# Layer 0 of a four-layer graph network in source order, with other numbers of buffers

## The chip, the cores and the metric

The kernel runs on one core of one Trainium2 chip. The metric is the device time of one execution in microseconds. TensorE (PE) multiplies matrices into PSUM, VectorE (DVE) does elementwise work and reductions, ScalarE (ACT) does activations and copies, GpSimd (POOL) issues the indirect gathers, and SyncE (SP) issues most of the other loads. Each engine works through its own queue in order. ACT issues stores as well.

## The reference, cut to what matters

A graph of 12,500 nodes with 64 features and 212,500 edges passes through four layers: a graph attention layer (layer 0), three graph convolutions (layer 1), five rounds of an edge network (layer 2) and a mean aggregation (layer 3). A residual sum and a normalization follow each. Layer 0 is this:

```python
h = (x @ W).reshape(n, HEADS, CH)                      # 4 heads of 16
e = leaky_relu(a_src[src] + a_dst[dst], 0.2)           # one value per edge and head
m = segment_max(e, dst); e = exp(e - m[dst])
s = segment_sum(e, dst)
out = segment_sum(h[src] * (e / s[dst])[:, :, None], dst)
y = layernorm(x + out + bias) * gamma + beta           # then layernorm(x + y)
```

Each self loop is added as an edge of its own.

## The kernel before

The nodes are cut into 128 windows of 98 (`NQ`, `QB`). The edges that end in a window lie in 128 x 16 slots: 14 columns hold rows gathered by matmuls with one-hot matrices and stored to DRAM beforehand, two hold overflow rows that POOL gathers. Windows go in groups of four (`G`). First the edges are sorted into slots and the rows for layer 0 are gathered; then the layers follow, each in a phase with its own pools of buffers.

For each window d, layer 0 does the following.

- `fetch` loads the gathered rows `hg` (one SP load and two POOL gathers). The features and the source's attention terms of every edge are in it.
- `place` builds the one-hot matrix of slots against nodes in two halves (`h32` on VectorE, a copy `hot` in FP8 on ScalarE, stored to `hot_d`), multiplies the attention terms by the edge's rank among those of its node (`rh`, `rv`) and adds them up per node and rank in PSUM (`prank`, 8 matmuls per half). TensorE runs a float32 matmul as two instructions, so the trace has 16 per half.
- `largest`, once per group, takes the largest attention value of each node from `prank`, the number of edges, and the term of the self loop (`pself`).
- `attend` builds the other one-hot matrix (`ot`), spreads the largest value back over the edges (`pd`, 16 matmuls), forms the exponent in a chain of small VectorE instructions (`ad`, then four on `z`), takes Exp on ScalarE, and multiplies the rows: `msg`.
- `add_up_whole` turns `hot` to float32 (`o32`, ScalarE) and adds up the messages per node in PSUM (`pacc`, 16 matmuls).
- `node0`, once per group, divides, adds the residuals, normalizes twice, and makes the table of layer 1: transposes and a dense matmul on TensorE (`pnode`), `tnew` on VectorE, then for each of the four windows a gather block (42 matmuls into `pgat`, two copies to `hb` on ScalarE, stores to `g_d`).
- `pump(6)` has POOL gather six columns of edge attributes for layer 2, which TensorE transposes (`pattr`) and ScalarE copies and stores.

POOL and SP follow the order of the source everywhere in the network. In layer 0 and layer 2, PE, ACT and DVE follow an order that a planner sets when the program is built, from a cost model of its own; in layers 1 and 3 they follow the source order (`tc.manual_schedule`). The source of layer 0 has `place` for window d, then `attend` and `add_up_whole` for window d-4, and at the end of a group the whole of `node0` and of `largest`. A layer 1 pass (`run_pass`) works in steps: each step does its window and then one piece of each node generator that is going.

Buffer numbers are given with the tiles: `hg` 9 in layer 0 (`hgbufs`), 7 in layers 1 and 2, 6 in layer 3; `hb` 2 in layer 0 (`hbbufs`), 4 later; the table `tnew` 2; `pacc`, `pd` and `prank` one each.

Of the kernel before, what the change touches and what calls it, by code (L numbers as in the profile page):

```python
# [865 lines left out]
def tile_gnn_resnorm_d4(ctx: ExitStack, tc: tile.TileContext, a: dict, out: bass.AP):  # L866
# [455 lines left out]
    def network():  # L1322
        with ExitStack() as s0:
# [77 lines left out]
            def inv_sqrt(val, shape, name):  # L1401
                sd = nw.tile(shape, F32, name=name + "_s")
                r = nw.tile(shape, F32, name=name + "_r")
                sca.activation(sd, val, AF.Sqrt)
                v.reciprocal(r, sd)
                v.tensor_mul(sd, r, r)
                v.tensor_mul(sd, sd, val)
                v.tensor_scalar(sd, sd, -0.5, 1.5, op0=OP.mult, op1=OP.add)
                v.tensor_mul(r, r, sd)
                return r  # L1410

            def layernorm(y, dst, gamma=None, beta=None):
                s = nw.tile([QB, G], F32, name="ln_sum")
                v.tensor_reduce(out=s, in_=y, axis=AX.X, op=OP.add)
                v.tensor_scalar(s, s, -1.0 / D, None, op0=OP.mult)
                v.tensor_tensor(y, y, s[:, :, None].to_broadcast([QB, G, D]), op=OP.add)
                sq = nt("ln_sq", bufs=1)
                v.tensor_mul(sq, y, y)
                va = nw.tile([QB, G], F32, name="ln_var")
                v.tensor_reduce(out=va, in_=sq, axis=AX.X, op=OP.add)  # L1420
                v.tensor_scalar(va, va, 1.0 / D, LN_EPS, op0=OP.mult, op1=OP.add)
                r = inv_sqrt(va, [QB, G], "ln")
                rb = r[:, :, None].to_broadcast([QB, G, D])
                if gamma is None:
                    v.tensor_tensor(dst, y, rb, op=OP.mult)
                else:
                    v.tensor_tensor(y, y, rb, op=OP.mult)
                    v.tensor_tensor(y, y, wide(gamma), op=OP.mult)
                    v.tensor_tensor(dst, y, wide(beta), op=OP.add)
# [103 lines left out]
            def add_up_whole(hot, x, ps):  # L1533

                nj = NJ // 2
                for hf in range(2):
                    o32 = wk.tile([P, nj, P], F32, name="o32", bufs=o32bufs)
                    sca.copy(o32, hot[:, hf * nj:hf * nj + nj, :])
                    for j in range(nj):
                        pe.matmul(ps, lhsT=o32[:, j, :], rhs=x[:, hf * nj + j, :], start=(hf + j == 0),  # L1540
                                  stop=(hf == 1 and j == nj - 1))
# [68 lines left out]
            def table():  # L1610
                return nw.tile([QB, 3, G, D], F32, name="tnew")
# [14 lines left out]
            hgbufs, ohbufs, hbbufs, o32bufs = 2 * G + 1, G + 2, 2, 2  # L1626
# [6 lines left out]
            def place(d, i, pk, hg, hot):  # L1633


                rh = wk.tile([P, RANKS, NJ], BF16, name="rh", bufs=1)
                v.tensor_tensor(rh, rk[:, d, None, :].to_broadcast([P, RANKS, NJ]), iotr, op=OP.is_equal)
                nj = NJ // 2
                for hf in range(2):
                    js = slice(hf * nj, hf * nj + nj)  # L1640
                    h32 = wk.tile([P, nj, P], F32, name="h32", bufs=3)
                    v.tensor_tensor(h32, dl[:, d, js][:, :, None].to_broadcast([P, nj, P]),
                                    iotb[:, None, :].to_broadcast([P, nj, P]), op=OP.is_equal)
                    sca.copy(hot[:, js, :], h32, saturate=False)
                    rv = wk.tile([P, nj, RANKS * H + 1], F32, name="rv")
                    v.tensor_tensor(rv[:, :, :RANKS * H].rearrange("p j (r h) -> p j r h", h=H),
                                    rh[:, :, js].rearrange("p r j -> p j r")[:, :, :, None].to_broadcast([P, nj, RANKS, H]),
                                    hg[:, js, D:][:, :, None, :].to_broadcast([P, nj, RANKS, H]), op=OP.mult)
                    v.memset(rv[:, :, RANKS * H:], 1.0)  # L1649
                    for j in range(nj):  # L1650
                        pe.matmul(pk[:, i // 2, i % 2, :RANKS * H + 1], lhsT=h32[:, j, :], rhs=rv[:, j, :],  # L1651
                                  start=(hf + j == 0), stop=(hf == 1 and j == nj - 1))
                sca.dma_start(hot_d[d], hot.rearrange("p j e -> p (j e)").bitcast(F32))
# [29 lines left out]
            def attend(hg, db, a3):  # L1683
                ot = wk.tile([QB, NJ, P], BF16, name="ot", bufs=1)
                v.tensor_scalar(ot, db, pcol[:QB], None, op0=OP.is_equal)
                pd = ps_tile([P, NJ, 3, 2 * H], "pd")
                for j in range(NJ):
                    pe.matmul(pd[:, j, :, :], lhsT=ot[:, j, :], rhs=a3, start=True, stop=True)
                ad = wk.tile([P, NJ, 2 * H], F32, name="ad")
# [8 lines left out]
                sca.activation(msg[:, :, D:], z, AF.Exp)  # L1698
                v.tensor_tensor(heads(msg[:, :, :D]), heads(hg[:, :, :D]),  # L1699
                                msg[:, :, D:][:, :, :, None].to_broadcast([P, NJ, H, C]), op=OP.mult)  # L1700
                return msg

            def node0(g, xsum, acc, ps, t0, x0):
# [13 lines left out]
                layernorm(y, y2, gamma0, beta0)  # L1717
                v.tensor_add(y2, y2, x0)
                x1 = nt("x1")
                layernorm(y2, x1)  # L1720
                deg = nw.tile([QB, G], F32, name="deg4")
                v.tensor_scalar(deg, cnt[:, sl], 1.0, None, op0=OP.add)
                v.tensor_copy(dinv[:, sl], inv_sqrt(deg, [QB, G], "dg"))
                for _ in conv(g, x1, ws1[0], 0, (x_d, x1)):
                    pass
# [33 lines left out]
            def load_db(d):  # L1759
                db = wk.tile([QB, NJ, P], BF16, name="db", bufs=3)  # L1760
# [3 lines left out]
            held = []  # L1764
# [3 lines left out]
            for d in range(NQ + G):  # L1768

                g, i = divmod(d, G)  # L1770
                if d + G - 1 < NQ:
                    held.append([fetch(d + G - 1, DH, g0_d, t0_d)])
                if d < NQ:
                    if i == 0:
                        pk = ps_tile([P, G // 2, 2, 256], "prank")
                    hot = wk.tile([P, NJ, P], F8, name="hot", bufs=G + 2)
                    held[d].append(hot)
                    place(d, i, pk, held[d][0], hot)
                    pump(6)
                if G - 2 <= d < NQ + G - 2:  # L1780
                    held[d - G + 2].append(load_db(d - G + 2))
                if d >= G:
                    if i == 0:
                        t0 = state(t0_d, g - 1, "t0", DH)
                        x0 = nt("x0")
                        load_x(x0, G * (g - 1))
                        xsum = nt("xsum", DH)
                    if i == 0:
                        ps = ps_tile([P, G, DH], "pacc")
                    hg, hot, db = held[d - G]  # L1790
                    add_up_whole(hot, attend(hg, db, a3[:, :, i]), ps[:, i, :])
                    if i == G - 1:
                        node0(g - 1, xsum, ps, pself, t0, x0)
                if d < NQ and i == G - 1:
                    a3, pself = largest(g, pk)
# [3 lines left out]
            hgbufs, ohbufs, hbbufs = AHEAD + 3, 2 * G, 4  # L1799
# [206 lines left out]
```

## Time and profile before

| | |
|---|---|
| Time, median of 11 runs | 11348.07 us (11321.43 to 11371.93) |
| The profiled execution: its time, its span | 11338.61 us, 11336.7 us |
| Busy: PE, DVE, ACT, POOL | 77%, 77%, 32%, 55% |
| Mean granted TensorE clock | 0.866 |
| Layer 0, about 1650 to 3510 us | PE 85% busy, DVE 79%, ACT 49%, POOL 73%, DMA share 0.51 |
| Layer 1, about 3510 to 5640 us | PE 71%, DVE 65%, POOL 71%, DMA share 0.89 |
| Layer 2, about 5640 to 10660 us | PE 94%, DVE 82%, POOL 44%, DMA share 0.72 |

How to read it: a group of instructions is named by its line in the kernel, its engine, its operation and output<-input; a line can be that of a helper that several callers share. A row of stretches gives, for each engine, the busy time and the number of instructions, then the clock that TensorE was granted (1.00 is full speed), the mean busy share of the 16 DMA engines, and GB/s. A wait names the instruction that waited, the one that released it, the total in us, how often, and the longest. A timeline row gives start, duration, engine, line and operation. Releasers are inferred, so a wait for several things is put down to the last.

### The profile page before, as it was taken

Reading aid. Unit: us, or ns where it says so; the run is one execution under the profiler, and the core shown is the slowest. Engines: PE = TensorE matmul, PEld = TensorE weight load, DVE = VectorE, ACT = ScalarE, POOL = GpSimd, SP = SyncE. Lnnn points to the kernel's source line nnn. Section 1 sums busy time; section 2 is a strip of 40 time slices with the busy share of each in tenths; the row PEclk is TensorE's granted clock in tenths of the full one; section 3 lists DMA queues with packets and bytes.
Section 4 is the critical chain, followed back from the end, with each engine's and each line's share of the span. In section 5 each row is a group of like instructions: output and inputs, shape, how many; then the busy total and the mean of one; then the engine's idle time right before and its main releaser. Section 6 shows DMA issues by size and latency. Waiting matters only on the chain.

```text
span 11336.7 us, 260322 instructions
## 1 busy us (share of the span) xinstructions
PE 8707.2 (77%) x101921; PEld 7312.9 (65%) x102115; DVE 8752.0 (77%) x16365; ACT 3652.6 (32%) x6423; POOL 6246.8 (55%) x4616
## 2 busy tenths in 40 slices
PE   2332468888886766677799999999998999898761
PEld 2110468888886666666677777777776777777551
DVE  6889447887775656667678878887887887888898
ACT  2341234544442222222233333333333333233200
POOL 0667578877765777776344434434443443444460
PEclk9855668988887888878799999999999999999885
DMA  2663684555456999988777767767776776767671
GB/s 79 223 225 105 190 255 136 171 149 154 146 154 192 291 283 294 294 266 276 233 246 233 238 211 239 237 203 248 236 237 212 238 238 197 244 226 236 202 231 51
DMA packets 1377992, 2414.81 MB, mean 213 GB/s; under 512 B 421097, under 2 KB 732537, under 8 KB 1376625
## 3 DMA queue, kind: packets, MB, share of 16 engines
q1 hardware_dynamic: 734770, 1565.65, 43.4%
q10 hardware_dynamic: 494495, 714.10, 17.5%
q0 software_dynamic: 147488, 118.29, 6.8%
q8 instruction: 808, 13.24, 0.5%
q14 instruction: 431, 3.53, 0.1%
HBM read 1655.94 MB, written 741.25 MB: 211 GB/s over the span
## 4 chain that ended last, share of the span: by engine, by line
PE 26%; DVE 14%; DMA 10%; issue 4%; ACT 2%; ACTq 1%; SPq 1%; POOL 0%; DVEq 0%; POOLq 0%
PE pacc L1530 7%; PE pe L1859 6%; PE p L1840 6%; PE pgat L931 4%; DVE msg L1524 3%; DMA hot<-hot_d 2%; DMA g_d<-hb 2%; DVE msg L1864 2%; DMA et<-at_d 1%; DVE hg L1524 1%; DVE eh L1439 1%; DMA oh<-oh_d 1%; DMA hg<-g_d 1%; ACT hb L932 1%; PE pe L1854 1%
## 5 line engine op out<-in xcount | busy, mean ns | idle before, releaser
L1496 POOL DMA_INDIRECT hg<-tq_d,q_ovr x2304 | 3378.1, 1466 | 3480.0 <-DVE msg L1864 1422.3
L959 POOL DMA_INDIRECT ag<-in_edge_attr_dram,q_eid x2048 | 2532.7, 1237 | 992.7 <-issue 573.6
L1530 PEld LDWEIGHTS <-hot 128*128 128x128 fp8e4 x18432 | 1715.0, 103 | 693.9 <-issue 538.3
L932 ACT COPY hb<-pgat 128x448 f32<-128x448 f32 (+1 forms) x2560 | 1301.2, 535 | 2172.7 <-PE pgat L931 1222.4
L931 PEld LDWEIGHTS <-oh 98*128 98x128 fp8e4 x48384 | 1751.4, 101 | 281.0 <-issue 255.9
L931 PE MATMUL pgat<-tnew,oh 98*128 98x64 bf16 x48384 | 1811.9, 198 | 151.7 <-ACT hb L932 104.0
L1524 DVE TENSOR_TENSOR msg<-msg 128x1024 f32<-128x1024 f32 x1280 | 1561.7, 1220 | 7.7
L1859 PEld LDWEIGHTS pe<-we,eh 128*128 128x128 f32 x10240 | 1364.2, 193 | 249.8 <-issue 116.1
L1859 PE MATMUL pe<-we,eh 128*128 128x128 f32 x10240 | 1478.9, 281 | 21.1 <-DVE eh L1439 8.6
L1438 ACT ACTIVATE eh<-p,be 128x512 f32<-128x512 f32 x1280 | 869.3, 687 | 1902.5 <-PE p L1840 1335.2
L1840 PE MATMUL p<-et,we 128*128 128x512 f32 x2560 | 1298.2, 609 | 123.0 <-DMA et<-at_d 67.6
L1524 DVE TENSOR_TENSOR hg<-hg 128x1024 f32<-128x1024 f32 x1024 | 1249.7, 1226 | 120.5 <-DMA hg<-tq_d,q_ovr 46.4
L1530 PE MATMUL pacc<-hg,hot 128*128 128x192 bf16 x8192 | 970.2, 282 | 360.8 <-DVE hg L1524 185.3
L1530 PE MATMUL pacc<-msg,hot 128*128 128x192 bf16 x10240 | 1042.6, 248 | 36.9 <-DVE msg L1524 26.6
L1864 DVE TENSOR_TENSOR msg<-pe,hg 128x512 f32<-128x512 f32 x1280 | 868.1, 686 | 243.0 <-PE pe L1859 233.4
L1439 DVE SCALAR_TENSOR_TENSOR eh<-eh 128x512 f32<-128x512 f32 x1280 | 862.5, 685 | 201.2 <-ACT eh L1438 200.9
L1651 PE MATMUL prank<-rv,h 128*128 128x161 f32 x4096 | 732.4, 336 | 128.9 <-DVE rv L1649 74.8
L1651 PEld LDWEIGHTS prank<-rv,h 128*128 128x128 f32 x4096 | 664.4, 216 | 143.6 <-DVE rv L1649 100.8
L1178 PE MATMUL taken<-sg,hotc 128*128 128x456 bf16 x512 | 245.3, 556 | 551.4 <-ACT sg L1175 447.1
L1840 PEld LDWEIGHTS p<-et,we 128*128 128x128 f32 x2560 | 427.9, 194 | 340.9 <-issue 139.1
L1540 PE MATMUL pacc<-msg,o 128*128 128x68 f32 x4096 | 580.3, 309 | 76.0 <-DVE msg L1699 74.9
L1540 PEld LDWEIGHTS pacc<-msg,o 128*128 128x128 f32 x4096 | 564.5, 224 | 88.8 <-DVE msg L1699 65.4
(321 smaller groups left out, 9724.8 us busy)
## 6 DMA issues: line engine op xcount, KB each, us to landing
hg<-g_d SPq DMA_DIRECT2D x1152, 448.0 KB
g_d<-hb ACTq DMA_DIRECT2D x1152, 416.0 KB
hot<-hot_d SPq DMA_DIRECT2D x1152, 256.0 KB
oh<-oh_d SPq DMA_DIRECT2D x1152, 171.5 KB
et<-at_d SPq DMA_DIRECT2D x640, 256.0 KB
vb<-vw_d SPq DMA_DIRECT2D x128, 912.0 KB
hg<-g_d SPq DMA_DIRECT2D x128, 476.0 KB
g_d<-hb ACTq DMA_DIRECT2D x128, 442.0 KB
```

The lines of the kernel that those rows point to most:

```text
L931: pe.matmul(ps[:, j, :], lhsT=oh[:, 7 * hf + j, :], rhs=t3(k), start=(k == 0), stop=(k == 2))
L932: sca.copy(hb[:, 7 * hf:7 * hf + 7, :], ps)
L959: pool.indirect_dma_start(out=ag[:, j, :], out_offset=None, in_=a["edge_attr_32"], in_offset=bass.IndirectOffsetOnAxis(ap=eid[:, d, lo + j ...
L1439: v.scalar_tensor_tensor(dst, dst, 0.1, dst, op0=OP.mult, op1=OP.max)
L1496: pool.indirect_dma_start(out=hg[:, NG + i, :], out_offset=None, in_=tab, in_offset=bass.IndirectOffsetOnAxis(ap=ovr[:, d, i:i + 1], axis= ...
L1524: v.tensor_tensor(x[:, k + 1], x[:, k], top[:, k], op=OP.subtract)
L1530: pe.matmul(ps.rearrange("p (k f) -> p k f", k=3), lhsT=hot[:, j, :], rhs=top[:, :, j, :], start=(j == 0), stop=(j == NJ - 1))
L1540: pe.matmul(ps, lhsT=o32[:, j, :], rhs=x[:, hf * nj + j, :], start=(hf + j == 0), stop=(hf == 1 and j == nj - 1))
L1651: pe.matmul(pk[:, i // 2, i % 2, :RANKS * H + 1], lhsT=h32[:, j, :], rhs=rv[:, j, :], start=(hf + j == 0), stop=(hf == 1 and j == nj - 1))
L1840: pe.matmul(p1.rearrange("p q e -> p (q e)"), lhsT=w["we1"][:, j].rearrange("p t d -> p (t d)"), rhs=et, start=True, stop=True)
L1859: pe.matmul(ps[:, u:u + 2, :].rearrange("p t d -> p (t d)"), lhsT=h1[j][:, (2 * hf + q) * P:(2 * hf + q + 1) * P], rhs=w["we2"].rearrange( ...
L1864: v.tensor_tensor(msg[:, half, :], ps, hg[:, half, :], op=OP.mult)
```

## The change

Layer 0's phase runs PE, ACT and DVE in source order, and its source becomes a loop of steps. Step d fetches for window d+3, places window d, makes the messages of window d-5 and the sums of window d-6, and runs one piece of every node generator that is going. `place`, `attend`, `node0` and the normalization become generators with yields, so that their parts can be laid between each other: `attend`'s `ot` and `pd` come before the first half of `place`, `ad`, `z` and Exp between the halves, and `msg` after them; the sums come after the node pieces. `o32` is made at the start of the step. The two `rv` tiles are fixed, and their column of ones is written once instead of twice in each window.

`table` has three buffers for `tnew` (in every layer that uses it); in layer 0 `hb` has three (two before), `hot` seven (six), `oh` five (six), `db` two (three). In layers 1 and 2 `hb` has six buffers (four before) and `hg` six (seven).

```diff
@@ layernorm, now layernorm_steps
-                r = inv_sqrt(va, [QB, G], "ln")
+                sd = root(va, [QB, G], "ln")
+                yield
+                r = inverse(sd, va, [QB, G], "ln")
@@ add_up_whole
-                    o32 = wk.tile([P, nj, P], F32, name="o32", bufs=o32bufs)
-                    sca.copy(o32, hot[:, hf * nj:hf * nj + nj, :])
...
+            def whole_hot(hot):
+                nj = NJ // 2
+                o32 = [wk.tile([P, nj, P], F32, name="o32", bufs=2) for _ in range(2)]
+                for hf in range(2):
+                    sca.copy(o32[hf], hot[:, hf * nj:hf * nj + nj, :])
+                return o32
@@ table
-                return nw.tile([QB, 3, G, D], F32, name="tnew")
+                return nw.tile([QB, 3, G, D], F32, name="tnew", bufs=3)
@@ layer 0
-            hgbufs, ohbufs, hbbufs, o32bufs = 2 * G + 1, G + 2, 2, 2
+            hgbufs, ohbufs, hbbufs = 2 * G + 1, G + 1, 3
...
+            rvs = [wk.tile([P, NJ // 2, RANKS * H + 1], F32, name=f"rv{hf}", bufs=1) for hf in range(2)]
+            for rv in rvs:
+                v.memset(rv[:, :, RANKS * H:], 1.0)
...
@@ node0
-                layernorm(y, y2, gamma0, beta0)
+                yield from layernorm_steps(y, y2, gamma0, beta0)
...
-                layernorm(y2, x1)
...
-                v.tensor_copy(dinv[:, sl], inv_sqrt(deg, [QB, G], "dg"))
-                for _ in conv(g, x1, ws1[0], 0, (x_d, x1)):
-                    pass
+                sd = root(deg, [QB, G], "dg")
+                yield from layernorm_steps(y2, x1)
+                v.tensor_copy(dinv[:, sl], inverse(sd, deg, [QB, G], "dg"))
+                yield from conv(g, x1, ws1[0], 0, (x_d, x1))
@@ the loop
+            phase.enter_context(tc.manual_schedule(engines={PE, ACT, DVE}))
+            room["hold"] = lambda ins: ins
...
+            while d < NQ + G + 2 or going:
+                at, up = d - G - 1, d - G - 2
                 if d + G - 1 < NQ:
                     held.append([fetch(d + G - 1, DH, g0_d, t0_d)])
+                if 0 <= at + 1 < NQ:
+                    dbs[at + 1] = load_db(at + 1)
+                if d % G == 0 and G <= d <= NQ:
+                    a3, pself = largest(d // G - 1, pk)
+                if 0 <= up < NQ:
...
+                    o32 = whole_hot(held[up][1])
...
+                    msgs = attend(held[at][0], dbs.pop(at), now[:, :, at % G])
+                    next(msgs)
...
+                    halves = place(d, pk, held[d][0], hot)
+                    next(halves)
+                if msgs is not None:
+                    next(msgs)
+                if halves is not None:
+                    next(halves)
+                    next(halves, None)
+                if msgs is not None:
+                    sent.append(next(msgs))
+                for t in list(going):
+                    if next(t, going) is going:
+                        going.remove(t)
+                if 0 <= up < NQ:
+                    if up % G == 0:
+                        acc = ps_tile([P, G, DH], "pacc")
+                    add_up_whole(o32, sent.pop(0), acc[:, up % G, :])
+                if 0 <= up < NQ and up % G == G - 1:
+                    going.append(node0(up // G, nt("xsum", DH), acc, own, t0, x0))
+                if d < NQ:
                     pump(6)
...
@@ layers 1 and 2
-            hgbufs, ohbufs, hbbufs = AHEAD + 3, 2 * G, 4
+            hgbufs, ohbufs, hbbufs = AHEAD + 2, 2 * G, 6
```

## The prediction

> **What bounds the kernel now.** I first read the busy time in stretches, which separates the layers. Layer 0 runs from about 1650 to 3510 us, layer 1 to 5640, layer 2 to 10660.
>
> ```profile
> core 0: us, PE busy (x) PEld busy (x) DVE busy (x) ACT busy (x) POOL busy (x), PEclk, DMA share, GB/s
> ...
> 1650.00:3510.00 1860.00, 1572.03 (x15925) 1522.10 (x15926) 1476.60 (x3644) 906.21 (x1243) 1350.53 (x1024) 0.85 0.51 148
> ...
> 3510.00:4080.00 570.00, 384.29 (x6305) 363.06 (x6303) 340.48 (x421) 132.97 (x293) 435.69 (x372) 0.81 0.90 285
> ...
> 5640.00:10660.00 5020.00, 4693.85 (x53252) 3713.25 (x53442) 4128.13 (x7607) 1684.44 (x3044) 2185.32 (x1283) 0.97 0.72 228
> ```
>
> In layer 0 TensorE is busy 85%, VectorE 79%, and POOL 1350.5 us plus 0.30 us ahead of each of 1024 gathers, 1657 us or 12.95 us per window. No engine is full; DMA, at 0.51, has room. Layer 1 (second row) is near its DMA bound at 0.90; layer 2 (third) is bound by TensorE. The pace of layer 0 comes from the view of one line, the placing matmul:
>
> ```profile
> L1651 PE MATMUL prank<-rv,h x4096: 297/301/637, 1670.9 to 3445.6; 128*128 128x161 f32 x196
> ```
>
> 128 windows in 1774.7 us: 13.87 us each, 55.5 us per group of four. That must be beaten.
>
> Next the timeline of VectorE, in layer 0 and then in layer 1, which already runs in source order:
>
> ```profile
> 2508.11 0.22 DVE L1692 TENSOR_TENSOR z<-hg,ad 128x64 f32<-128x64 f32 x1
> 2508.25 0.42 DVE L1429 TENSOR_TENSOR y<-y,q_beta 98x256 f32<-98x256 f32 x1
> 2508.58 0.22 DVE L1693 SCALAR_TENSOR_TENSOR z<-z 128x64 f32<-128x64 f32 x1
> 2508.72 0.42 DVE L1718 TENSOR_TENSOR y<-y,x 98x256 f32<-98x256 f32 x1
> ```
> ```profile
> 5100.18 0.42 DVE L1416 TENSOR_TENSOR y<-y,ln_sum 98x256 f32<-98x256 f32 x1
> 5100.64 0.42 DVE L1418 TENSOR_TENSOR ln_sq<-y 98x256 f32<-98x256 f32 x1
> 5101.10 0.42 DVE L1420 TENSOR_REDUCE ln_var<-ln_sq 98x4 f32<-98x256 f32 x1
> 5101.55 0.17 DVE L1421 TENSOR_SCALAR ln_var<-ln_var 98x4 f32<-98x4 f32 x1
> ```
>
> The planner lays a message chain (z) and a normalization chain (y) into each other, and an instruction starts 0.08 us before the one ahead ends. Where each uses the result of the one ahead, the pitch is duration plus 0.04 us (0.46 for 0.42). Source order has the second form. Last, the waits, in layer 0 and then in layer 1 (3560 to 4640 us); columns are total, times, longest:
>
> ```profile
> DVE ad L1690 <- PE pd L1688: 79.2, 38, 14.0
> ...
> DVE tnew L1734 <- PE pnode L1398: 8.0, 14, 1.1
> ```
> ```profile
> DVE tnew L1734 <- PE pnode L1398: 242.7, 46, 8.4
> ...
> ACT hb L932 <- DMA g_d<-hb: 120.4, 27, 7.3
> ```
>
> The same wait, VectorE's tnew for the dense matmul, is 0.6 us a time under the planner and 5.3 us a time in source order.
>
> **Layer 0, VectorE's own time.** Durations are means of the groups by line. A step has ot 0.76, rh 0.48, two h of 1.22, two rv of 1.48, ad 0.55, four z of 0.21, msg 1.22: 9.26 us in 12 instructions, of which four follow-ons depend (+0.04) and eight do not (-0.08): 8.78 us. largest: 13 instructions, 4.14 us, ten dependent: 4.30. Node pieces by the same count: first 5.04, second 4.96, third 2.48, the table (tnew and two cuts) 1.26; together 13.74. The two removed memsets (0.065 each) are worth 0.5 us a group, and are left out of these counts. A group: 4 x 8.78 + 4.30 + 13.74 = 53.2 us, against 1476.6 / 32 = 46.1 now. So reordering alone takes back 7 us, since it puts dependent instructions side by side.
>
> The Trainium skill, "VectorE: DVE Perf Modes", section "The DRAIN you can't avoid", says that a semaphore between chained operations costs nothing extra. By that VectorE would keep about 45.6 us a group, and the path below, whose VectorE part is 40.3 us, would shrink to about 60 us. The two timelines above differ by 0.12 us per instruction, and I keep 53.2.
>
> **Layer 0, the path through one group.** In each step PE's queue holds, in this order: pd, first half of placing, second half, the pieces' matmuls (a gather block; in one step the transposes, in one the dense matmuls), the sums, the attribute transposes. VectorE's queue: largest (one step in four), ot, rh, first h and rv, ad and z, second h and rv, msg, the pieces. Two waits follow. VectorE's ad needs pd, which stands behind the sums of the step before; behind ad are queued the whole rest of placing and so PE's second half. And in the step that makes a table, tnew needs the dense matmuls, behind the second half of placing and a gather; behind it stands the first node piece of the next group.
>
> PE's pieces at full clock, from timelines: half of placing 2.35 us (16 in 2.42 at 2504.5), sums 3.68, gather 1.40, pd 0.55, dense 0.90, transposes 0.50, attributes 0.27 on average. At half clock: 4.13, 5.54, 2.04, and dense 1.53. Means of layer 0: 2.86, 4.53, 1.63, 0.57, 1.13, 0.52.
>
> Steps counted by d modulo 4. Step 3 and step 0 are VectorE's: 8.78 + 4.96, then 4.30 + 3.62 (ot to first rv) + 4.10 (ad to second rv): 25.76. Step 0 to 1 on PE: half of placing, gather, sums, attributes, pd: 2.86 + 1.63 + 4.53 + 0.27 + 0.57 = 9.86. VectorE ad to second rv: 4.10. Step 1 to 2 on PE, with the transposes: 10.38. VectorE: 4.10. PE half of placing, gather, dense: 5.62. VectorE's table and first piece: 1.26 + 5.04 = 6.30. Sum 66.1 us a group; 61.9 at full clock, 73.6 at half. Of it VectorE waits about 13 us.
>
> Which clock? Stretches of 1 us:
>
> ```profile
> 2508.00:2509.00 1.00, 0.00 (x0) 0.00 (x0) 1.00 (x5) 0.00 (x0) 0.69 (x2) 1.00 0.29 58
> ...
> 2511.00:2512.00 1.00, 1.00 (x6) 1.00 (x5) 1.00 (x2) 1.00 (x1) 0.81 (x1) 0.50 0.09 11
> ...
> 2515.00:2516.00 1.00, 1.00 (x11) 1.00 (x11) 1.00 (x7) 0.00 (x0) 0.69 (x2) 1.00 0.05 7
> ```
>
> After about 2.5 us without a matmul (2507.3 to 2509.8) the clock was 0.50 for some 3.5 us. The path has four gaps of 1.7 to 2.5 us a group, so I take the layer's present means, near layer 1's 0.81. The Trainium skill, "TensorE: Matmul & The Clock Gate", section "Why this matters for your kernels", puts the drop at idle gaps above about 3 us; by that the sum would be the full-clock 61.9, which these rows do not bear out.
>
> The first five steps have no messages and go at POOL's 12.95 us; 122 intervals go at 66.1 / 4 = 16.5 instead of 13.87: +324, and -4 for the first five. The end has six steps without placing, about 8 us each, and a chain of pieces, against 88 us now from the last placing to layer 1: +5. Layer 0: +325 us (bounds +197 and +553).
>
> **What costs nothing.** ScalarE has 7.1 us of work a step; its o32 copies wait for the sums of the step before, but its Exp is done 2 us before msg wants it, under the second h and rv. If that cover went, a step would lose up to the 1.28 us of a table load. SP and POOL keep their order. A fetch waits for the message of one step ago; the rows are used three steps later. db has two buffers and a lead of one step, some 16 us.
>
> **Buffers later.** Six hb buffers: in layer 1 ScalarE waited 120.4 us for stores in 1080 us; at a DMA share of 0.90 at most 0.10 x 1140 = 114 us of the two first passes can be won. Six hg buffers instead of seven: SP's loads there already waited 180 us for the sums; up to 90 us more. I take -10, nearer to nothing because DMA is full. Layer 2: its order is planned anew; PE is 93.5% busy at a clock of 0.97, so I take 0, with 1% (50 us) either way.
>
> **Sum.** The profiled execution took 11338.6 us (span 11336.7), 9.5 below the median of 11348.1. 11338.6 + 325 - 10 + 9.5 = 11663, rounded to 11660.
>
> **Rivals.** *VectorE full, the two waits hidden.* If PE reaches pd and the dense matmuls before VectorE asks, layer 0 costs 53.2 us a group: 122 x (13.3 - 13.87) = -70, with -10: 11270. It decides where the two waits together stay under 55.5 - 53.2 = 2.3 us a group. For it: tnew's 0.6 us now. Against: layer 1's 5.3 us. Chance 0.14. *Half clock.* If each gap halves the clock through the next bursts, +553: 11890. Against: 0.81 in layer 1 at 67% busy. Chance 0.09. *No change*: layer 0 at full clock and without dependent pitches, about +150, paid back by 114 in layer 1 and a little of layer 2: within 20 us of 11350. Chance 0.03. The forecast has 0.74, spread 11480 to 11840.
>
> The range 11400 to 11930 takes in full clock with the best of the buffers and most of the half clock; it leaves out the two low cases and a little above. Faster by over 0.2% (23 us, about what a measurement of this kernel can tell) 0.14, within 0.03, slower 0.83.
>
> **What would show it.** Right: placing matmuls spread over about 2080 us; VectorE about 1620 us busy in layer 0 (the 0.04 us behind a dependent instruction is not busy time); waits of ad for pd of 2 to 6 us, two per group, and of tnew for pnode of 4 to 6 us once per group; a clock of 0.80 to 0.87. Wrong: ad and tnew without waits, or a pace under 13.87 us; or layer 1 or 2 moving by over 100 us.

## The result, and the profile after

The changed kernel takes 11472.08 us (median of 8 runs, 11457.1 to 11479.79); the kernel before took 11343.82 us beside it (31 runs). The ratio is 1.0112, 95% interval 1.0102 to 1.0123: slower by 128 us, in the forecast's direction and inside its range, but well under the 312 us forecast.

The profiled execution has a span of 11463.1 us against 11336.7. Where the 126 us lie is read from the first and last start of three groups, in the view of one line or tile: the placing matmul (its line of before is in the prediction), the sums of gathered rows, whose first start opens layer 1 (before, L1530; after, L1542), and VectorE's message product of layer 2 (before, L1864; after, L1913).

```profile
L1671 PE MATMUL prank<-rv,h x4096: 297/301/637, 1669.5 to 3627.8; 128*128 128x161 f32 x196
```
```profile
L1530 PE MATMUL pacc<-hg,hot x8192: 244/247/368, 3544.9 to 11100.6; 128*128 128x192 bf16 x200
```
```profile
L1542 PE MATMUL pacc<-hg,hot x8192: 244/248/368, 3749.3 to 11226.8; 128*128 128x192 bf16 x200
```
```profile
L1864 DVE TENSOR_TENSOR msg<-pe,hg x1280: 661/685/702, 5700.8 to 10619.6; 128x512 f32<-128x512 f32 x183
```
```profile
L1913 DVE TENSOR_TENSOR msg<-pe,hg x1280: 652/685/699, 5918.9 to 10747.6; 128x512 f32<-128x512 f32 x183
```

Placing takes 1958.3 us in place of 1774.7. Layer 1's first sum of gathered rows starts at 3749.3 in place of 3544.9, so layer 0 costs 204 us. Layer 2's messages take 4829 us in place of 4919: 90 us are won there. Layer 1, from that sum to layer 2's first message, takes 2170 us in place of 2156, and the rest 1.6 less. The sum is 204 + 14 - 90 - 2 = 126.

The stretches that answer to those shown of before, layer 0, the start of layer 1, and layer 2:

```profile
core 0: us, PE busy (x) PEld busy (x) DVE busy (x) ACT busy (x) POOL busy (x), PEclk, DMA share, GB/s
1650.00:3650.00 2000.00, 1578.17 (x15413) 1534.94 (x15412) 1614.82 (x3288) 870.74 (x1196) 1484.35 (x1024) 0.81 0.46 135
3739.00:4309.00 570.00, 389.87 (x6442) 368.46 (x6442) 361.08 (x437) 136.81 (x295) 451.11 (x391) 0.82 0.93 291
5850.00:10800.00 4950.00, 4678.50 (x53394) 3715.12 (x53586) 4134.15 (x7629) 1695.82 (x3049) 2221.01 (x1291) 0.98 0.73 232
```

In layer 0 the clock fell from 0.85 to 0.81, and no engine is full. VectorE's waits from 1700 to 3580 us (total, times, longest):

```profile
DVE ad L1713 <- PE pd L1710: 168.4, 60, 12.6
DVE tnew L1758 <- PE pnode L1398: 114.4, 28, 5.1
```

These are the two waits of the forecast's path: some two of ad per group, 2.8 us each, and one of tnew, 4.1 us. In VectorE's timeline a dependent instruction starts 0.04 us after the end of the one ahead (0.46 us from start to start for a length of 0.42), and the wait of tnew stands in front of the table:

```profile
2562.48 0.42 DVE L1439 TENSOR_TENSOR y<-y,ln_r 98x256 f32<-98x256 f32 x1
2562.94 0.42 DVE L1440 TENSOR_TENSOR y<-y,q_gamma 98x256 f32<-98x256 f32 x1
...
2610.70 0.42 DVE L1758 TENSOR_TENSOR tnew<-pnode,q_dinv 98x256 f32<-98x256 f32 x1 [5.12 <-PE pnode L1398]
```

Since ad, tnew and ot keep their places in source order, the forecast's path can be measured leg by leg, as means over 29 groups of the timeline. The prediction's terms are summed to the same marks.

| leg of a group | forecast us | measured us |
|---|---|---|
| ot of step 3 to ad of step 0 (VectorE) | 8.78 + 4.96 + 4.30 + 3.62 = 21.66 | 21.62 |
| ad of step 0 to ad of step 1 (VectorE, then PE) | 4.10 + 9.86 = 13.96 | 11.92 |
| ad of step 1 to ad of step 2 (VectorE, then PE) | 4.10 + 10.38 = 14.48 | 13.22 |
| ad of step 2 to tnew (VectorE, then PE) | 4.10 + 5.62 = 9.72 | 9.34 |
| tnew to ot of step 3 (VectorE) | 1.26 + 5.04 = 6.30 | 6.69 |
| group | 66.1 | 62.8 |

VectorE's legs fit; what is short is PE's. PE's timeline of one group (start, length, instructions joined, and in brackets the idle time before) shows why:

```profile
2574.55 6.39 PE L1671 MATMUL prank<-rv,h 128*128 128x161 f32 x32 [2.42 <-DVE rv L1667]
2580.78 1.40 PE L931 MATMUL pgat<-tnew,oh 98*128 98x64 bf16 x42
2582.02 3.76 PE L1556 MATMUL pacc<-msg,o 128*128 128x68 f32 x32
...
2590.36 3.30 PE L1671 MATMUL prank<-rv,h 128*128 128x161 f32 x16 [1.89 <-DVE rv L1667]
2593.46 2.20 PE L931 MATMUL pgat<-tnew,oh 98*128 98x64 bf16 x42
2595.50 0.50 PE L1390 MATMUL pnode<-q_ident,x 98*64 98x98 f32 x4
2595.83 3.71 PE L1556 MATMUL pacc<-msg,o 128*128 128x68 f32 x32
...
2613.08 7.06 PE L1556 MATMUL pacc<-msg,o 128*128 128x68 f32 x32 [2.42 <-DVE xsum L1732]
2619.94 0.63 PE L1710 MATMUL pd<-adm,ot 98*128 98x24 bf16 x16
2621.04 7.04 PE L1671 MATMUL prank<-rv,h 128*128 128x161 f32 x32 [0.47 <-DVE rv L1667]
```

The sums that ad waits for take 3.7 us, at full speed; those at 7.06 us, at half clock, run in the step where VectorE is at its node pieces and nobody waits for them. In the same 29 groups the sums take 3.76 us in step 0, 3.71 in step 1, 7.07 in step 2 and 3.76 in step 3. The forecast put the layer's mean, 4.53, on the path.

Some slow bursts do stand on the path. In the group shown the second half of placing took 3.30 us in step 1 and 3.77 in step 2, with gathers of 2.20 and 1.77, where 2.47 and 1.40 are full speed. That is so in 11 of the 29 groups, and these take about 64.6 us; 17 others take 61.1 to 62.0.

### The profile page after: what moved, and what is told of

It is laid out like the page before. It is cut to its first block, busy times and chain, and to the rows that moved or that the text cites. A ratio compares the mean times of both kernels' runs of the same rounds, so it can differ in the third digit from the quotient of the medians.

```text
span 11463.1 us, 259539 instructions
## 1 busy us (share of the span) xinstructions
PE 8740.6 (76%) x101921; PEld 7367.3 (64%) x102115; DVE 8919.7 (78%) x16111; ACT 3653.8 (32%) x6411; POOL 6389.1 (56%) x4616
## 3 DMA queue, kind: packets, MB, share of 16 engines
q8 instruction: 807, 13.22, 0.5%
## 4 chain that ended last, share of the span: by engine, by line
PE 27%; DVE 16%; DMA 11%; issue 5%; ACT 1%; POOL 1%; ACTq 1%; SPq 0%; POOLq 0%; DVEq 0%
PE pacc L1542 8%; PE pe L1908 6%; PE p L1889 5%; PE pgat L931 5%; DVE msg L1536 4%; DMA hot<-hot_d 3%; DMA g_d<-hb 3%; DVE msg L1913 2%; DMA ag<-in_edge_attr_dram,q_eid 2%; DVE hg L1536 2%; DVE eh L1451 2%; DMA hg<-g_d 2%; PE pe L1903 1%; PE pnode L1398 1%; ACT hb L932 1%
## 5 line engine op out<-in xcount | busy, mean ns | idle before, releaser
L959 POOL DMA_INDIRECT ag<-in_edge_attr_dram,q_eid x2048 | 2694.4, 1316 | 990.9 <-issue 581.1
L1542 PEld LDWEIGHTS <-hot 128*128 128x128 fp8e4 x18432 | 1727.6, 103 | 686.9 <-issue 519.4
L1542 PE MATMUL pacc<-hg,hot 128*128 128x192 bf16 x8192 | 991.2, 286 | 346.3 <-DVE hg L1536 165.8
L1542 PE MATMUL pacc<-msg,hot 128*128 128x192 bf16 x10240 | 1041.9, 248 | 45.9 <-DVE msg L1536 31.3
L1913 DVE TENSOR_TENSOR msg<-pe,hg 128x512 f32<-128x512 f32 x1280 | 868.0, 685 | 234.4 <-PE pe L1908 230.7
L1671 PE MATMUL prank<-rv,h 128*128 128x161 f32 x4096 | 771.3, 355 | 225.1 <-DVE rv L1667 206.7
L1671 PEld LDWEIGHTS prank<-rv,h 128*128 128x128 f32 x4096 | 723.0, 232 | 247.6 <-DVE rv L1667 155.0
L1560 DVE TENSOR_REDUCE xsum<-pacc 98x128 f32<-98x384 f32 x576 | 318.6, 553 | 507.3 <-PE pacc L1542 507.0
```

The lines of the kernel that those rows point to most:

```text
L959: pool.indirect_dma_start(out=ag[:, j, :], out_offset=None, in_=a["edge_attr_32"], in_offset=bass.IndirectOffsetOnAxis(ap=eid[:, d, lo + j ...
L1542: pe.matmul(ps.rearrange("p (k f) -> p k f", k=3), lhsT=hot[:, j, :], rhs=top[:, :, j, :], start=(j == 0), stop=(j == NJ - 1))
L1913: v.tensor_tensor(msg[:, half, :], ps, hg[:, half, :], op=OP.mult)
```

## Experiments: layer 0

Three theories stood. The forecast's: layer 0 pays for source order through the two waits, and the gain behind it belongs to the later buffers. A rival: the path is not what counts, VectorE is simply full with its dependent pairs. Another: the layers disturb one another through the buffers, so neither part has a price of its own.

**Source order alone.** The changed kernel with the table and the later buffers as before:

```
-                return nw.tile([QB, 3, G, D], F32, name="tnew", bufs=3)
+                return nw.tile([QB, 3, G, D], F32, name="tnew")
...
-            hgbufs, ohbufs, hbbufs = AHEAD + 2, 2 * G, 6
+            hgbufs, ohbufs, hbbufs = AHEAD + 3, 2 * G, 4
```

> The changed kernel with two table buffers, seven hg and four hb buffers in layers 1 and 2 as before: layer 0 in source order alone. Theories A and B: layer 0 as in the changed kernel (placing spread over 1958 us, layer 1 starting some 205 us later), layer 2 back at 4910 to 4930, so 200 to 220 us slower than before. Theory C: layer 2 stays at 4829, so 115 to 130 us slower.

Measured: 11535.87 us against 11331.01, ratio 1.0186 (1.0168 to 1.0204): +205 us. Placing runs from 1659.7 to 3619.8, and layer 2's messages take 4910 us. The two parts add: some 200 us for layer 0, and 90 back in layer 2.

**One wait taken away.** The table is made a step after the dense matmuls, so that tnew no longer asks while they stand behind placing. One line in conv, for layer 0 alone:

```
+                if also is not None:
+                    yield
```

> The changed kernel with tnew (and with it the rest of the table and the gathers) a step after its dense matmul; the wait of ad for pd is left. Path theory: VectorE's wait of 4.1 us a group for pnode goes and nothing takes its place before the next step's first half of placing, so layer 0 is 95 to 130 us shorter than in the changed kernel (placing spread over 1830 to 1865 us), the whole 0 to 30 us slower than before. Rival (the freed time goes to the wait for pd, since PE's sums of that step are what comes next): layer 0 shorter by less than 50 us, and ad waits by 2 to 4 us more a group.

Measured: 11350.92 us against 11337.24, ratio 1.001 (1.0001 to 1.002). Placing takes 1846 us, 112 less than in the changed kernel, which is 3.5 us for each of 32 groups: most of tnew's wait of 4.1 us. VectorE's waits from 1700 to 3580 us have lost tnew, and ad's are there as before:

```profile
DVE ad L1713 <- PE pd L1710: 187.6, 73, 12.6
```

So the time is a path's, and a wait on it costs nearly what it lasts.

**Both waits moved.** Besides the table, ot and pd of the next window are issued at the end of a step, ahead of the sums, so that pd is long done when ad asks:

```
+                if 0 <= at + 1 < NQ:
+                    asked.append(attend(held[at + 1][0], dbs.pop(at + 1), now[:, :, (at + 1) % G]))
+                    next(asked[-1])
                 if 0 <= up < NQ:
                     ...
                     add_up_whole(o32, sent.pop(0), acc[:, up % G, :])
```

> The changed kernel with both waits of the path moved: ot and pd of the next window are issued at the end of a step, ahead of the sums, so that ad no longer stands behind them; and tnew is taken a step after its dense matmul. Path theory: the waits of ad for pd (5.6 us a group) and of tnew for pnode (4.1 us a group) fall under 1 us each, a group goes from 62.5 to 53 to 55 us, layer 0 loses 230 to 290 us, the whole is 100 to 160 us faster than before. Rival (POOL paces): in the changed kernel its eight gathers take (1.57 + 0.30) x 6 + (1.09 + 0.30) x 2 = 14.0 us a step, 56 us a group; then layer 0 loses 180 to 210 us and VectorE waits for hg instead. Rival (the waits come back elsewhere, as Exp behind the o32 copies or PE behind VectorE): less than 100 us gained on the changed kernel, with new waits of msg or rv of over 4 us a group.

Measured: 11639.27 us against 11331.01, ratio 1.0277 (1.0262 to 1.0292): 308 us over the kernel before, where the changed kernel is 128 over it. Placing takes 2114 us. Waits of all engines from 1700 to 3380 us:

```profile
ACT o L1550 <- PE pacc L1556: 364.6, 98, 7.9
DVE msg L1723 <- ACT msg L1721: 328.1, 96, 9.8
...
PEld L1710 <- DVE ot L1707: 297.9, 72, 6.1
```

The wait of ad fell to 27.5 us in this stretch, and three others took its place; they form a ring through in-order queues. The sums stand on PE behind pd, which waits for ot, now VectorE's last instruction of a step. ScalarE's o32 copies need buffers that those sums free. Exp stands on ScalarE behind the copies, and VectorE's msg waits for Exp. The prediction had named Exp's cover, 2 us, and priced its loss at up to 1.28 us a step; it cost 328.1 / 96 = 3.4 us a time. From 1700 to 3400 us the clock was 0.73.

**The ring opened.** The next window's ot and pd come right behind msg, ahead of the node pieces; the o32 copies behind Exp and the casts; the six steps of loads ahead of the pieces. The table stays a step later.

```
                     sent.append(next(msgs))
+                if 0 <= at + 1 < NQ:
+                    ...
+                    next(asked[-1])
+                if d < NQ:
+                    pump(6)
+                if 0 <= up < NQ:
+                    o32 = whole_hot(held[up][1])
                 for t in list(going):
```

> The run with both waits moved was 167 us slower than the changed kernel: msg waited 390 us for Exp, which stood on ScalarE behind the o32 copies of sums that stood on PE behind a pd that waited for an ot issued last. Here the same two moves, with ot and pd right behind msg, o32 behind Exp and the casts, and the attribute transposes ahead of the pieces, so that no queue holds an early need behind a late one. Path theory: ad, tnew and msg wait under 1.5 us a group together, a group takes 53 to 55 us, layer 0 is 210 to 280 us shorter than in the changed kernel, the whole 80 to 150 us faster than before. Rival (POOL paces at 14.0 us a step, 56 us a group): layer 0 170 to 210 us shorter, VectorE waits for hg. Rival (in-order queues always pass the wait on): layer 0 less than 100 us shorter.

Measured: 11237.84 us against 11337.24, ratio 0.9914 (0.9902 to 0.9927): faster than both kernels. Placing takes 1728.3 us, and from step 5 on 13.81 us a step, 55.2 a group. That is the rival "VectorE full, the two waits hidden", whose price was 53.2 us a group; msg's waits for Exp, 60 us in some 30 groups, make up the other 2 us. VectorE's waits from 1700 to 3380 us, and the stretch from 1700 to 3400:

```profile
DVE msg L1723 <- ACT msg L1721: 60.0, 32, 9.9
DVE ad L1713 <- PE pd L1710: 2.7, 2, 1.8
```
```profile
1700.00:3400.00 1700.00, 1356.74 (x15064) 1314.93 (x15063) 1568.98 (x3199) 841.21 (x1163) 1391.70 (x1001) 0.91 0.53 153
```

VectorE is busy 92%, and the clock rose to 0.91. But POOL, with 1391.7 us and about 0.30 us ahead of each of 1001 gathers, has no room either, so which of the two sets the pace was open.

**Which engine is the bound.** First hb was put back to four buffers in layers 1 and 2 (`hbbufs` 6 to 4):

> The kernel with the queues in turn (the next window's one-hot and degree matmul right behind msg, o32's copies behind Exp and the casts, the table a step later, six steps of loads ahead of the node pieces), with hb at four buffers in layers 1 and 2 in place of six. With hb six in layer 2 alone the kernel before took 4908 us there against 4919, and no difference in all, so by the theory that hg's number alone moves layer 2: 11225 to 11250 us, layer 0's placing 1728 +-10, layer 2 4825 to 4840. The rival, that hb's spare buffers carry some of the gain once the loads are fewer: 20 to 50 us longer in layer 2.

Measured: 11233.33 us against 11325.37, ratio 0.9917 (0.9896 to 0.9938); placing 1726.8 us, layer 2 4827. The spare hb buffers carry nothing. Beside it the same with the two reciprocal-root chains of the third node piece interleaved, the same instructions in another order:

```
+                for sd, val, r in both:
+                    v.reciprocal(r, sd)
+                for sd, val, r in both:
+                    v.tensor_mul(sd, r, r)
...
-                yield from layernorm_steps(y2, x1)
-                v.tensor_copy(dinv[:, sl], inverse(sd, deg, [QB, G], "dg"))
+                other = [sd, deg]
+                yield from layernorm_steps(y2, x1, other=other)
+                v.tensor_copy(dinv[:, sl], other[2])
```

> The same with hb four, and in the third node piece the two chains of dependent small VectorE instructions (the reciprocal root of the variance and that of the degree) interleaved. A dependent neighbour costs 0.12 us more than an independent one (length +0.04 against length -0.08), and some eight pairs a group are parted: about 0.9 us x 32 groups, 25 to 35 us less in layer 0 if VectorE sets the pace there (busy 1569 of 1700 us). The rival, POOL sets it (busy 1392 of 1700 us with 1001 instructions, and 0.30 us between two): 0 to 10 us less.

Measured: 11208.59 us, ratio 0.9896 (0.9874 to 0.9917), the fastest of all: 117 us under the kernel before and 24.7 under its neighbour. Placing takes 1699.8 us, 27 less, 0.84 us a group where 0.9 was expected. So VectorE sets the pace, and not POOL, and a dependent pair parted is worth about 0.1 us there (0.84 us over some eight pairs).

## Experiments: what shortened layer 2

**All later buffers, and the table.** Two kernels carry the change's later parts on the kernel before, the first with hg six and hb six, the second with hg six and three table buffers:

```
-            hgbufs, ohbufs, hbbufs = AHEAD + 3, 2 * G, 4
+            hgbufs, ohbufs, hbbufs = AHEAD + 2, 2 * G, 6
```

> The kernel before with six hb and six hg buffers in layers 1 and 2 (hg seven, hb four before), nothing else changed. The changed kernel's layer 2 took 4829 us from the first to the last message, against 4919 before, and its layer 1 13 us more. Theory A (the six hb and six hg buffers did both): layer 2 at 4815 to 4845 us, layer 1 10 to 15 us longer, so the whole 70 to 85 us faster (ratio 0.993). Theory B (the third table buffer did it): layer 2 at 4910 to 4930, the whole 0 to 20 us slower. Theory C (the planner's order of layer 2 differs only because it starts from another layer 0): as B.

```
-                return nw.tile([QB, 3, G, D], F32, name="tnew")
+                return nw.tile([QB, 3, G, D], F32, name="tnew", bufs=3)
...
-            hgbufs, ohbufs, hbbufs = AHEAD + 3, 2 * G, 4
+            hgbufs, ohbufs, hbbufs = AHEAD + 2, 2 * G, 4
```

> The kernel before with three table buffers and six hg buffers (the third table does not fit beside seven), hb at four. Theory B (third table buffer): layer 2 shorter by 80 to 100 us, the whole faster by 60 to 90. Theory A with hb as its cause: layer 2 at 4910 to 4930, layer 1 0 to 20 us longer, the whole within 20 us of before. Theory A with hg as its cause: as theory B, and then e1 is faster too.

Then each alone: hg six (`AHEAD + 3` to `AHEAD + 2` in the same line), and hb six in layer 2 (a line `hbbufs = 6` ahead of it).

> The kernel before with six hg buffers in layers 1 and 2 instead of seven, and nothing else. Layer 2 took 4919 us before, 4829 in the changed kernel, 4827 with six hg and six hb, 4836 with six hg and three tables. Theory A-hg (six hg buffers alone shorten layer 2, through the order that the planner then finds): layer 2 at 4825 to 4840, layer 1 unchanged, the whole 70 to 95 us faster than before. Theory A-other (six hb and the third table each do it on their own, hg does nothing): layer 2 at 4910 to 4930, the whole within 15 us of before.

> The kernel before with six hb buffers in layer 2 alone, hg at seven. Theory A-hg: layer 2 at 4900 to 4930, the whole within 20 us of before. Theory A-other: layer 2 at 4825 to 4840, the whole 70 to 95 us faster. Layer 1 is as before by either.

| kernel before with | us | ratio (95%) | layer 2, us |
|---|---|---|---|
| hg six, hb six | 11263.9 | 0.9941 (0.9927 to 0.9954) | 4826 |
| hg six, three tables | 11253.81 | 0.9935 (0.9917 to 0.9953) | 4835 |
| hg six | 11264.25 | 0.9933 (0.992 to 0.9946) | 4826 |
| hb six in layer 2 | 11325.24 | 0.9994 (0.9984 to 1.0004) | 4905 |

One buffer of gathered rows less is the whole effect. The prediction expected layer 2's order to be planned anew; with hg six alone every engine's instructions stand in the same order as before, and in the changed kernel's layer 2 VectorE's and ScalarE's do too. The waits of ScalarE for loads in layer 2 (5760 to 10480 us), and of PE's weight load for ScalarE's eh, first before, then with hg six:

```profile
ACT hb L932 <- DMA hot<-hot_d: 55.1, 17, 6.2
ACT hb L932 <- DMA hg<-g_d: 50.8, 26, 3.7
...
PEld p L1840 <- ACT eh L1438: 119.7, 154, 4.2
```
```profile
ACT hb L932 <- DMA hg<-g_d: 17.2, 12, 4.0
ACT hb L932 <- DMA hot<-hot_d: 7.7, 3, 2.8
...
PEld p L1840 <- ACT eh L1438: 52.2, 117, 1.4
```

ScalarE's hb copies waited 106 us on the loads of hot and hg and now 25, and PE, the engine that bounds this layer, waits for eh 68 us less in its weight loads and 49 less in its matmuls (52.4 to 3.7).

**Time or place.** Six buffers might help because the loads go out later, or because the tiles behind lie elsewhere. Five in layer 2 alone, and six with an unused tile that fills the seventh's room:

```
+            hgbufs = AHEAD + 1
```

> The kernel before with five buffers of gathered rows (hg) in layer 2 alone, seven still in layer 1. With six alone, in both layers, layer 2's messages took 4826 us in place of 4919, with every instruction in the same order on every engine, so either the time at which a load goes out or the place of the tiles in SBUF did it. Theory T (loads that go out later collide less with the rest): layer 2 as with six or shorter still, 4800 to 4840, in all 75 to 120 us less than before. If the loads then come too late, ACT's hb waits for hg's DMA above the 55 us that they took in layer 2 of before and the gain shrinks. Theory P (place): any length between 4800 and 4930, not tied to the loads' times.

```
+            hgbufs = AHEAD + 2
+            pad = wk.tile([P, NJ, D], F32, name="hgpad", bufs=1)
+            v.memset(pad, 0.0)
```

> The kernel before with six buffers of gathered rows in layer 2 alone, and beside them an unused tile of one buffer's size, filled once, so that the tiles behind lie where seven buffers put them. Theory T (the times of the loads): layer 2 4820 to 4840 us, in all 75 to 95 us less than before. Theory P (the tiles' place in SBUF): layer 2 back at 4905 to 4930, in all within 15 us of before. In layer 1 nothing is changed: 2164 to 2193 us by either.

Measured: with five 11263.4 us, ratio 0.9944 (0.9924 to 0.9964), layer 2 4855 us, longer than expected; ScalarE's hb copies wait 43 us for the loads of hot and hg, 25 with six, and another load has come late, that of the one-hot rows oh (5 us with six):

```profile
ACT hb L932 <- DMA oh<-oh_d: 100.9, 46, 4.6
```

So five is past the best. With six and the pad 11244.27 us, 0.9923 (0.9904 to 0.9942), layer 2 4830. The place is refuted; it is when the loads may go out. From the issue of hg's load to the message product that uses it there are 48.6 us before, 40.8 with six buffers, 41.0 with six and the pad, and 34.0 with five (medians over the 640 windows).

**Is it SP's queue?** Before, SP waits 177 us in layer 2 between hg's load and hot's for the sums of an older step; with hg six 9 us. Ten hot buffers take the wait away with hg seven; seven bring it back with hg six; and hot's load ahead of hg's turns the order (`hotbufs["n"]` is the number of hot buffers, `AHEAD + 4` in the kernel before):

```
+            hotbufs["n"] = AHEAD + 6      # hg seven
```

> The kernel before (hg seven) with ten hot buffers in layer 2 in place of eight. Theory H (SP, with hg's load of a step already out, waits for the sums of an older step to free a hot buffer, and hot, et and the next loads go out late): the 177 us of L1504's waits for pacc fall under 20, and layer 2 comes to 4825 to 4850 us, in all 70 to 95 us less than before. Rival (hg's earlier load itself crowds the DMA engines): the wait goes, layer 2 stays at 4905 to 4930.

```
+            hotbufs["n"] = AHEAD + 3; hgbufs = AHEAD + 2
```

> The kernel before with hg six and, in layer 2, seven hot buffers in place of eight. Theory H: the wait of L1504 for pacc is back, over 150 us, and layer 2 at 4900 us or more, so no gain over the kernel before or a loss. Rival (hg's earlier load is the cause): layer 2 stays at 4820 to 4850.

```
-                    asked.append((fetch(d, D, gd, tab), load_hot(d), extra(d)))
+                    hot = load_hot(d); asked.append((fetch(d, D, gd, tab), hot, extra(d)))
```

> The kernel before (hg seven, hot eight) with hot's load issued ahead of hg's in layer 2. By theory H the queue is held at hot as before, now with hg behind it: layer 2 4890 to 4930 us. Rival (hot only comes late because it stands behind hg's wait for its own store): ACT's waits for hot's DMA, 55 us in layer 2, go and layer 2 takes 4840 to 4870.

Ten hot buffers: the wait is gone, yet 11314.45 us, ratio 0.9985 (0.9976 to 0.9994), layer 2 4912. Seven with hg six: 11236.71 us, 0.9918 (0.9905 to 0.9931), layer 2 4830, although SP waits again (the kernel before first, then this one):

```profile
SPq L1504 <- PE pacc L1530: 177.0, 117, 2.9
```
```profile
SPq L1504 <- PE pacc L1530: 173.9, 122, 2.9
```

So the held queue is not the cause, in both directions. Hot ahead of hg: 11382.03 us, 1.005 (1.0036 to 1.0063), layer 2 4965, against both expectations; SP then waits 1290.6 us for the sums with hg behind it. What is left is how early a window's loads go out. With ten hot buffers hg's load is out 48.5 us ahead of its use, as before; with seven and hg six 41.1. But hot's load, and that of the edge attributes (et), stand behind hg's in SP's queue and follow within 2 us (hot goes out 47.9 us ahead before and 40.4 with hg six; put ahead of hg's, 50.4), so they move with it, and no run tells which of them must go out later. The traces record no landings. How an earlier load lengthens the layer was not isolated, and stays open.

**And in layer 1?** Over all runs so far layer 1 takes 2128 to 2165 us (mean 2151) in eight kernels with seven hg buffers there, and 2163 to 2184 (mean 2171) in nine with six, whatever hb has. So the fastest kernel was given seven in layer 1 and six in layer 2, for which the table's buffers go back to two, and was run beside itself:

```
-                return nw.tile([QB, 3, G, D], F32, name="tnew", bufs=3)
+                return nw.tile([QB, 3, G, D], F32, name="tnew")
...
-            hgbufs, ohbufs, hbbufs = AHEAD + 2, 2 * G, 4
+            hgbufs, ohbufs, hbbufs = AHEAD + 3, 2 * G, 4
...
+            hgbufs = AHEAD + 2      # ahead of layer 2
```

> The kernel with the queues in turn and the two chains interleaved, with hg seven in layer 1, six in layer 2 alone, and the table's buffers at two. If six buffers cost layer 1 what the spread of the runs suggests: layer 1 2140 to 2165 us in place of 2169, in all 5 to 30 us less than the same kernel beside it, 11180 to 11205 us. The rival, that the spread of layer 1 is scatter: no difference over 10 us. With two tables in place of three the dense matmul's table might wait for its buffer; then layer 0's placing rises above 1700 us by over 10.

> The kernel with the queues in turn, hb four and the two chains interleaved, again, beside the one with hg by layer: 11195 to 11225 us, layer 1 2165 to 2185 us if six buffers of hg set it there, anything from 2128 on if it is scatter.

These two ran on another chip, on which the kernel before took 12224.66 us, so only the ratios speak. By layer: 11998.51 us, 0.9809 (0.9783 to 0.9835); the same number throughout: 12040.68 us, 0.985 (0.9831 to 0.987). Layer 1 takes 2458 us against 2504, layer 2 4888 against 4887, placing 1998 against 1987. So the pair differs by 42 us, more than the 5 to 30 expected, and layer 1 alone by 46. The table's buffers differ between the two as well, and layer 1 uses the table; that number was not tried alone beside hg seven. With this reserve, seven suit layer 1 and six suit layer 2, and the change took six in both.

## Why the prediction was right or wrong

- **VectorE's pitch**: right. The VectorE legs measured 28.3 us against 28.0, busy time in layer 0 1614.82 against about 1620, and the interleaved chains gave 0.84 us a group for the 0.9 that the 0.12 us imply. The Trainium skill, "VectorE: DVE Perf Modes", section "The DRAIN you can't avoid", says that a semaphore between chained operations costs nothing extra; here an instruction that uses the result just ahead starts 0.12 us later than one that does not, and no run tells the semaphore from the dependence. The 45.6 us a group that the prediction drew from it are not borne out. That its sum, about 60 us, lies nearer to the 62.8 measured than 66.1 does comes from PE's legs.
- **The two waits**: right in kind and place. Tnew's was 4.1 us for a forecast 4 to 6, ad's 2.8 us for 2 to 6. The table made later gave back 112 us.
- **PE's pieces on the path**: the step that failed, "I take the layer's present means". The mean clock was 0.81, as forecast, but the path does not see the mean. The slow sums (7.07 us) stand in step 2 of every group, where VectorE is the later one; those on the path took 3.7 us for the 4.53 put there. The second half of placing and the gather of steps 1 and 2 were slow in 11 of 29 groups. So most groups ran near the 61.9 us that the prediction gave for full clock and set aside. Size: 122 intervals at 15.69 us in place of 16.53, 102 us.
- **The base pace**: 1774.7 us hold 127 intervals, not 128, so 13.97 us and not 13.87; 13 us too much. The first five steps went at 7.4 us and not at POOL's 12.95, 28 us. The other way, the last window's own placing took 6.8 us that the sum did not count, and the end, from the last placing to layer 1, cost 22 us and not 5: 24 us together.
- **Layer 2**: the other step that failed, "I take 0". It measured -90 us, outside the 50 us either way, and the reason given (a new order) was wrong: six hg buffers alone did it, in the same order. Together with PE's pieces this is about the whole miss of 184 us; the other terms nearly cancel.
- **Layer 1**: forecast -10 us (hb up to 114 won, hg up to 90 lost), measured +14. Hb six shows nothing in any run; hg six costs some 20 us by the means above, and 46 where the two were run side by side, with the table's buffers changed as well.
- **Rivals**: *VectorE full* did not happen, for the reason given (the waits were not hidden); its price proved right once they were: 55.2 us a group, 2 of them msg's wait, for 53.2. *Half clock* came on the path only in part, in 11 of 29 groups; its price took 5.54 us for the sums, a burst that is at half clock only in part, and wholly at half clock they take 7.07.

## What to carry to other kernels

On a path that crosses engines, take each piece's duration from the bursts that stand on the path, not from the layer's mean: the slowest may lie where nobody waits, as the sums of step 2 did here in every group. Moving a wait in a fixed order is worth about its length only if what is issued in its place stands in nobody's way; follow each in-order queue once around before moving it. A prefetch buffer more is not free: with the same order of instructions, one less made layer 2 some 2% shorter and layer 1 some 1% longer, so try it layer by layer.

## What the hardware showed unexpectedly

A PE gap of 1.9 us (2588.5 to 2590.4) was followed by a fall of the clock to 0.50, some 1.5 us after the work had resumed, for about 3.5 us; the Trainium skill, "TensorE: Matmul & The Clock Gate", section "Why this matters for your kernels", puts the limit at gaps above about 3 us.

```profile
2589.00:2590.00 1.00, 0.00 (x0) 0.00 (x0) 1.00 (x1) 0.98 (x1) 0.77 (x1) 1.00 0.00 0
...
2592.00:2593.00 1.00, 1.00 (x6) 1.00 (x5) 1.00 (x3) 0.00 (x0) 1.00 (x1) 0.50 0.65 96
...
2595.00:2596.00 1.00, 1.00 (x23) 1.00 (x21) 0.04 (x1) 0.66 (x2) 0.91 (x1) 0.89 0.85 228
2596.00:2597.00 1.00, 1.00 (x11) 1.00 (x11) 0.00 (x0) 0.23 (x1) 0.78 (x1) 1.00 1.05 260
```

But the same gap at the same place of the next group was not: the half of placing behind it took 2.47 us there, and 3.30 here.

```profile
2655.07 2.47 PE L1671 MATMUL prank<-rv,h 128*128 128x161 f32 x16 [1.89 <-DVE rv L1667]
2657.37 1.40 PE L931 MATMUL pgat<-tnew,oh 98*128 98x64 bf16 x42
```

From 1850 to 3600 us of the changed kernel, 55 gaps of 1.9 to 2.0 us began at full clock: after 22 of them the clock fell, 0.8 to 1.4 us behind the gap, and after 33 it did not. All 56 gaps of 2.4 us and more brought a fall, at the latest 0.2 us behind the gap. What decides about the short ones the runs don't show.

POOL's gathers of attributes took 1568 ns each in layer 0 of the changed kernel and 1320 before, while those of rows took 1097 and 1301. Nothing in them was changed, and the runs don't say why.

One chip took 7 to 8% longer for the same program (the kernel before 12224.66 us, the one with interleaved chains 12040.68). The latter moved 237 GB/s there in layer 1 (3900 to 6400 us) and 274 on the chip before (3490 to 5650), at a clock of 0.75 and 0.80. In layer 0 it took 17% longer to place, at 0.77 and 0.90, and in layer 2 1%. What differs between the chips the runs don't show.
